# Four matmuls on a tile of ones ahead of the first loaded block

## The chip, the cores and the metric

The kernel runs on one core of a Trainium2 chip. The metric is the device time of one execution in microseconds (us), and the median over executions is compared. One further execution is recorded by the hardware profiler; its times are what the views of the profile show. The engines are named as in the profile: PE (TensorE matmuls), PEld (TensorE weight loads, which overlap PE), DVE (VectorE), ACT (ScalarE), POOL (GpSimd) and SP (SyncE, which here only issues DMAs). A trailing q (SPq, ACTq) is an engine's instruction queue.

## The reference

The input x has 32 batches of 128 tokens with 128 features, in float32. Two layers are added to it, each a conditioned mixture of experts followed by a feed-forward part:

```
x = x + L0_ffn(L0_cond(x, cond))   # L0_cond: top 2 of 4 experts per batch, plus a shared expert
                                   # L0_ffn: 8 gated experts, all used, weighted per token
x = x + L1_ffn(L1_cond(x, cond))   # L1_cond: 2 shared experts, top 2 of 8 experts per token
                                   # L1_ffn: low rank (32) two-layer network
```

What matters around the change is the very first part that is computed, the shared expert of L0_cond:

```
shared = gelu(context_c @ sw1 + sb1, approximate=True) @ sw2 + sb2
```

with `sw1` of 128x512 and `sw2` of 512x128. All matrix products are done in float32.

## The kernel before

The tokens are held transposed, features on the 128 partitions, as eight blocks of 512 tokens (`NB`, `TB`). Two big SBUF tiles hold them for the whole run: `xall` for x and `c0all` for the output of L0_cond; `xT[b]` and `c0T[b]` are their slices of 512 columns. PSUM is one tile `banks` of eight banks of 512 columns. The first six (`NM`) are handed out in turn by `mm_tile`, the last two (`NY`) by `y_tile`; banks 6 and 7 hold sums over several matmuls.

The program first issues its loads, most on the SP queue and three on the ACT queue. The ones that matter here are at L156 to L163:

- L156 (ACT): the first 128 columns of `sw1`; L157 (SP) and L159 (ACT): the two halves of block 0 of x.
- L160 (SP): the other columns of `sw1`; L161 (ACT): `par`, one tile with all small constants and biases.
- L162 (SP): block 1 of x; L163 (SP): `sw2`; L165: blocks 2 to 7. After these come the weights of the later stages.

The work then goes block by block through `pipelined`, which starts the upward part of one unit before the downward part of the unit ahead of it:

- `shared_up(blk)`, L274: four chunks, each a matmul of 128x128 weights by 512 tokens (L279) into its own bank, evicted by ScalarE with gelu and a bias from `par` (L280). For the first two blocks VectorE also sums x over tokens (`sums`, L237), four blocks each.
- `shared_down(blk)`, L286: four matmuls that accumulate in one of banks 6 and 7 (L290), and an eviction by VectorE into `c0T[blk]` (L294).

In between, at points that the table `between` (L639) names, the gates of the conditioned experts are computed (`cond_gates`, L301; `schedule`, L350; `spread_slots`, L411). They are chains of small VectorE operations with small TensorE and ScalarE steps, and their result decides which expert weights are fetched (L471) and used by the 36 units of `unit_up` and `unit_down` (L514 to L546). Then come the eight-expert part (L714 to L761, matmuls L253 and L750), which is most of the time, and layer 1.

POOL fills the last columns of `c0all` (from block 5 on) with zeros at L651, and other constant tiles at L184 to L194. The program says what is to be done in what order on each engine, but a planner may reorder instructions of one engine unless they are kept in program order (`tc.keep_in_program_order`); it also derives from the tiles' regions who waits for whom. TensorE's first instruction in this kernel is the weight load of L279 for block 0.

Of the kernel before, what the change touches and what calls it, by code (L numbers as in the profile page):

```python
# [32 lines left out]
F32 = mybir.dt.float32  # L33
# [5 lines left out]
P = 128  # L39
B, S, D = 32, 128, 128  # L40
BB = 4
TB = BB * S
NB = B // BB
# [6 lines left out]
NHEAD = S // 3  # L50
# [48 lines left out]
def adaln_ffn(  # L99
# [3 lines left out]
    nc = tc.nc  # L103
    V = nc.vector
# [3 lines left out]
    apool = ctx.enter_context(tc.tile_pool(name="acts", bufs=1))  # L108
# [5 lines left out]
    NM, NY = 6, 2  # L114
    banks = psum.tile([P, NM + NY, TB], F32, tag="banks", name="banks", bufs=1)
# [18 lines left out]
    def const(shape, name, dtype=F32):  # L134
        return cpool.tile(shape, dtype, tag=name, name=name)


    par = const([P, NCOLS], "par")
    par32 = const([P, NCOLS32], "par32")
    rows = const([P, NROW], "rows")  # L140
# [3 lines left out]
    wu_t = wpool.tile([P, EF, H], F32, tag="wu", name="wu_t")  # L144
    wd_t = wpool.tile([P, EF, NC, D], F32, tag="wd", name="wd_t")


    xall = apool.tile([P, NB * TB + NHEAD], F32, tag="x", name="xall")
    c0all = apool.tile([P, NB * TB + NHEAD], F32, tag="c", name="c0all")
    xT = [xall[:, b * TB : (b + 1) * TB] for b in range(NB)]  # L150
    c0T = [c0all[:, b * TB : (b + 1) * TB] for b in range(NB)]
    ident = const([P, P], "ident")
# [1109 lines left out]
```

## Time and profile before

| What | Before |
|---|---|
| median of 3 runs | 967.09 us |
| lowest and highest run | 967.04 and 967.91 us |
| the profiled execution, its own time | 966.89 us |
| its span, first to last instruction | 965.1 us |
| time around the span | 1.79 us |
| PE busy | 951.8 us in 6138 passes |
| DVE busy | 593.5 us |
| ACT busy | 351.7 us |
| first matmul starts | 4.54 us |

A row of a timeline gives the start of a group of equal instructions, the time from its first start to its last end, the engine, the line of the code, what is written from what, the shape and the count. In brackets stands the idle time of the engine just before it and what ended that. Ends of matmuls are modelled, so the spacing of starts tells more than a duration does. A float32 matmul appears as two matmul instructions, each with a weight load; they are called passes here. In the window tables each row is a stretch of the span with the busy time and the count of instructions of each engine, the granted TensorE clock as a share of full speed, and the load of the DMA engines.

### The profile page before, as it was taken

To read this page: it belongs to the slowest core of one execution; us is meant where nothing else is said; L and a number is where in the kernel's file an instruction comes from. 1 tells how busy PE (TensorE), PEld (TensorE's weight loads), DVE (VectorE), ACT (ScalarE), POOL (GpSimd) and SP (SyncE) were. 2 spreads that over 40 slices of the span, in tenths; PEclk is the share of its full clock that TensorE was granted. 3 is DMA by queue.
4 is the path that set the end of the run, shared out by engine and by line. 5 is a ranking of instruction groups with operands and counts; after the bars stand their busy time and mean duration, and the time that the engine had idled before them with its cause. 6 is when DMAs were issued, how large, how long until landed. Compare 5 with 4: busy or idle time off the path is not lost.

```text
span 965.1 us, 15705 instructions
## 1 busy us (share of the span) xinstructions
PE 951.8 (99%) x6138; PEld 444.3 (46%) x6138; DVE 593.5 (61%) x1118; ACT 351.7 (36%) x622; POOL 75.1 (8%) x86
## 2 busy tenths in 40 slices
PE   8999999999999999999999999999999999999997
PEld 3588984444444444444444444444444443322333
DVE  4444574766866776686676887668667655633323
ACT  5355544223322322232232332223223223456674
POOL 0000001200101011010101011011010000000000
PEclk9999999999999999999999999999999999999999
DMA  9745641000000000000000000000000003040101
GB/s 315 245 143 171 213 138 48 2 1 4 1 1 2 1 1 1 1 1 1 2 2 1 1 2 3 1 2 1 1 1 1 1 1 89 1 91 1 45 2 45
DMA packets 22850, 38.13 MB, mean 40 GB/s; under 512 B 1968, under 2 KB 13232, under 8 KB 22768
## 3 DMA queue, kind: packets, MB, share of 16 engines
q1 hardware_dynamic: 22192, 36.48, 12.4%
q8 instruction: 53, 0.87, 0.4%
q10 hardware_dynamic: 576, 0.54, 0.2%
q14 instruction: 29, 0.24, 0.1%
HBM read 34.65 MB, written 2.36 MB: 38 GB/s over the span
## 4 chain that ended last, share of the span: by engine, by line
PE 84%; ACT 1%; DVE 0%; issue 0%; DVEq 0%; ACTq 0%
PE banks L253 57%; PE banks L750 20%; PE banks L890 3%; PE banks L290 1%; PE banks L984 1%; ACT hl L992 0%; PE banks L279 0%; PE banks L553 0%; PE banks L266 0%; PE banks L568 0%; PE banks L582 0%; DVE pg L978 0%; DVE pT L979 0%; ACT hs L280 0%; DVE fin L1176 0%
## 5 line engine op out<-in xcount | busy, mean ns | idle before, releaser
L667 ACT ACTIVATE sf<-banks 128x512 f32<-128x512 f32 x256 | 152.7, 597 | 435.3 <-PE banks L253 421.4
L668 DVE TENSOR_TENSOR hf<-sf,banks 128x512 f32<-128x512 f32 x256 | 174.8, 686 | 183.0 <-PE banks L253 182.2
L253 PE MATMUL banks<-c0all,wg_t 128*64 128x512 f32 x1024 | 263.5, 593 | 0.0
L253 PE MATMUL banks<-cg,wu_t 128*64 128x512 f32 x1024 | 263.1, 592 | 0.0
L253 PEld LDWEIGHTS banks<-cg,wu_t 128*64 128x64 f32 x1024 | 73.4, 137 | 146.3 <-issue 126.9
L253 PEld LDWEIGHTS banks<-c0all,wg_t 128*64 128x64 f32 x1024 | 72.8, 137 | 121.4 <-issue 108.8
L662 POOL PARTITION_BROADCAST fg<-fgT x64 | 72.7, 1149 | 655.1 <-DVE cg L711 493.6
L750 PE MATMUL banks<-t,wd_t 128*64 128x256 f32 x512 | 121.0, 379 | 0.0
L750 PE MATMUL banks<-hf,wd_t 128*64 128x256 f32 x512 | 104.2, 379 | 0.0
L750 PEld LDWEIGHTS banks<-hf,wd_t 128*64 128x64 f32 x512 | 53.4, 137 | 55.4 <-issue 36.8
L750 PEld LDWEIGHTS banks<-t,wd_t 128*64 128x64 f32 x512 | 70.1, 137 | 0.0
L524 ACT ACTIVATE h<-banks,w 128x256 f32<-128x256 f32 (+3 forms) x136 | 49.6, 433 | 49.4 <-PE banks L521 49.3
L750 PE MATMUL banks<-hf,a_sum 128*64 128x256 f32 x512 | 66.1, 379 | 0.0
L750 PE MATMUL banks<-t,a_sum 128*64 128x256 f32 x256 | 65.7, 379 | 0.0
L730 DVE TENSOR_TENSOR hf<-hf 128x512 f32<-128x512 f32 x64 | 63.0, 984 | 2.2
L253 PE MATMUL banks<-xall,rw_t 128*32 128x512 f32 x512 | 58.4, 593 | 0.2 <-ACT hl L992 0.2
L253 PE MATMUL banks<-xall,sws 128*32 128x512 f32 x512 | 57.4, 593 | 0.2 <-ACT hl L992 0.2
L537 PE MATMUL banks<-h,w 128*128 128x256 f32 (+3 forms) x272 | 52.5, 338 | 0.0
L521 PE MATMUL banks<-x,w 128*128 128x256 f32 (+3 forms) x272 | 52.2, 337 | 0.0
L521 PEld LDWEIGHTS banks<-x,w 128*128 128x128 f32 x272 | 45.3, 190 | 4.4 <-issue 1.0
L537 PEld LDWEIGHTS banks<-h,w 128*128 128x128 f32 x272 | 44.7, 190 | 4.1 <-issue 0.7
L965 ACT ACTIVATE hr<-banks 128x512 f32<-128x512 f32 x64 | 36.9, 591 | 25.6 <-PE banks L253 25.4
(211 smaller groups left out, 775.1 us busy)
## 6 DMA issues: line engine op xcount, KB each, us to landing
w<-in_experts SPq DMA_DIRECT2D x36, 514.5 KB
wg_t<-in_w_gate SPq DMA_DIRECT2D x8, 256.0 KB
wu_t<-in_w_up SPq DMA_DIRECT2D x8, 256.0 KB
wd_t<-in_w_down SPq DMA_DIRECT2D x8, 256.0 KB
gates<-rg SPq DMA_DIRECT2D x4, 512.0 KB
gates<-rg SPq DMA_DIRECT2D x8, 256.0 KB
xall<-in_x SPq DMA_DIRECT2D x7, 256.0 KB
out<-fin SPq DMA_DIRECT2D x6, 256.0 KB
```

The lines of the kernel that those rows point to most:

```text
L253: mm = nc.tensor.matmul(ps[own, :], lhsT=w[:, own], rhs=x, start=True, stop=True)
L290: nc.tensor.matmul(y, lhsT=sw2_t[:, c, :], rhs=h[:, c, :], start=(c == 0), stop=(c == NC - 1))
L521: nc.tensor.matmul(ps[c][:, :m, :n], lhsT=w1, rhs=x[:, :m, :n], start=True, stop=True)
L524: nc.scalar.activation(h[:, c, :m, :n], ps[c][:, :m, :n], AF.Gelu_apprx_tanh, bias=bias)
L537: nc.tensor.matmul(y[:, :m, :n], lhsT=w2, rhs=h[:, c, :m, :n], start=(c == 0), stop=(c == NC - 1))
L662: nc.gpsimd.partition_broadcast(bc, row)
L667: silu = nc.scalar.activation(s, ps_gate, AF.Silu)
L668: V.tensor_tensor(h, s, ps_up, ALU.mult)
L730: V.tensor_tensor(b12, b12, b11, ALU.subtract)
L750: nc.tensor.matmul(y[half, n], lhsT=w[:, c, :], rhs=h[:, c, :], start=first, stop=(e == EF - 1 and last))
L890: in_order(nc.tensor.matmul(y[32 * j : 32 * (j + 1)], lhsT=w, rhs=h, start=first, stop=last))
L965: in_order(nc.scalar.activation(h[:, at, :], ps, AF.Gelu))
```

## The change

Ahead of all loads in the program, the two tiles `xall` and `c0all` are allocated (they were allocated a few lines further down), VectorE writes ones into the first 256 columns of `c0all`, and TensorE multiplies them four times: the weights are the first 128 of these columns, the moving side all 256, and the result goes to the first half of PSUM bank 7 (`NM + 1`). Nobody reads it. The first real matmul into bank 7, in the second block's `shared_down`, starts a new sum. The 256 columns of `c0all` are later overwritten with the real values by L294.

```diff
+    xall = apool.tile([P, NB * TB + NHEAD], F32, tag="x", name="xall")
+    c0all = apool.tile([P, NB * TB + NHEAD], F32, tag="c", name="c0all")
+
+    V.memset(c0all[:, : TB // 2], 1.0)
+    for _ in range(4):
+        nc.tensor.matmul(
+            banks[:, NM + 1, : TB // 2], lhsT=c0all[:, :P], rhs=c0all[:, : TB // 2], start=True, stop=True
+        )
+
     par = const([P, NCOLS], "par")
...
-    xall = apool.tile([P, NB * TB + NHEAD], F32, tag="x", name="xall")
-    c0all = apool.tile([P, NB * TB + NHEAD], F32, tag="c", name="c0all")
     xT = [xall[:, b * TB : (b + 1) * TB] for b in range(NB)]
```

## The prediction

> **What bounds the kernel now.** I read the page first: the span, busy times and slices.
>
> ```profile
> span 965.1 us, 15705 instructions
> PE 951.8 (99%) x6138; PEld 444.3 (46%) x6138; DVE 593.5 (61%) x1118; ACT 351.7 (36%) x622; POOL 75.1 (8%) x86
> PEclk9999999999999999999999999999999999999999
> ```
>
> TensorE is busy for 951.8 of 965.1 us. Of the 13.3 us of idle time the view of PE's waits puts 4.5 us in one place, the first matmul, which waits for the first block of x. Whatever shortens TensorE's stream anywhere shortens the whole, unless a later wait is tied to something that does not move with it. So I went next to the first microseconds, in the timeline (start, duration, engine, line, operands; in brackets the idle time before and what ended it).
>
> ```profile
> 0.73 0.19 POOL L184 MEMSET ones<- 32x128 f32 x1 [0.29 <-POOLq L1248]
> ...
> 1.00 1.40 POOL L651 MEMSET c0all<- 128x1578 f32 x1
> ...
> 4.50 0.33 DVE L237 TENSOR_REDUCE hd<-xall 128x4 f32<-128x168 f32 x1 [4.50 <-DMA xall<-in_x]
> 4.51 0.50 PEld L279 LDWEIGHTS banks<-xall,sw_t 128*128 128x128 f32 x2 [4.51 <-issue]
> 4.54 7.79 PE L279 MATMUL banks<-xall,sw_t 128*128 128x512 f32 x13 [4.54 <-DMA xall<-in_x]
> ```
>
> Engines are released from the start barrier at about 0.73 us. From then to 4.50 VectorE and TensorE have nothing to do: the gap that the change fills. Then the timeline of the weight loads alone, for the pace of the first real matmuls. A float32 matmul goes as two passes, each with one weight load, and in the steady stream a load starts when the pass before it starts.
>
> ```profile
> 5.53 0.34 PEld L279 LDWEIGHTS banks<-xall,sw_t 128*128 128x128 f32 x1 [0.52 <-issue]
> 6.38 0.34 PEld L279 LDWEIGHTS banks<-xall,sw_t 128*128 128x128 f32 x1 [0.52 <-issue]
> 7.23 0.34 PEld L279 LDWEIGHTS banks<-xall,sw_t 128*128 128x128 f32 x1 [0.52 <-issue]
> 8.09 0.34 PEld L279 LDWEIGHTS banks<-xall,sw_t 128*128 128x128 f32 x1 [0.52 <-issue]
> 8.73 0.19 PEld L279 LDWEIGHTS banks<-xall,sw_t 128*128 128x128 f32 x1 [0.31 <-issue]
> 9.16 0.19 PEld L279 LDWEIGHTS banks<-xall,sw_t 128*128 128x128 f32 x1 [0.24 <-issue]
> 9.59 0.19 PEld L279 LDWEIGHTS banks<-xall,sw_t 128*128 128x128 f32 x1 [0.24 <-issue]
> ```
>
> The pace is 0.853 us a pass up to 8.09 and 0.429 from 8.73 on: half speed, then full. The pass from 8.09 to 8.73 took 0.64, so it is about half of each, and the rise is at 8.09 + 0.42 = 8.51. The first pass began at 5.53 - 0.853 = 4.68, so TensorE worked 3.83 us at half speed and **lost 1.92 us**. Check: the 17th load is at 13.02, so fifteen passes took 8.34 us, where 15 x 0.429 = 6.44; the difference is 1.90. The PEclk row says full speed all along, so it doesn't show this; it does show a fall at the other end, in the table of windows (width, PE busy, PEld, DVE, ACT, POOL, PEclk, DMA):
>
> ```profile
> 964.00:964.50 0.50, 0.00 (x0) 0.00 (x0) 0.00 (x0) 0.00 (x0) 0.00 (x0) 0.74 0.00 0
> 964.50:965.10 0.60, 0.00 (x0) 0.00 (x0) 0.00 (x0) 0.00 (x0) 0.00 (x0) 0.50 0.00 0
> ```
>
> An idle TensorE goes back to exactly half; 0.74 is 0.24 us at full and 0.26 at half speed, so the fall is at 964.24, 3.6 us after the last matmuls began to drain (960.68).
>
> **The change part by part.** Nothing is removed. Added are one VectorE memset of 128x256 and four float32 matmuls of 256 columns, that is eight weight loads and eight passes (6138 + 8 of each). Two tiles are allocated earlier, with no instruction.
>
> *The memset.* VectorE is idle until 4.50, so it is hidden. No VectorE memset is in the trace. Below, it can't be less than 0.14 us, what L333 takes for 32x4; above, 0.43, what L597 takes for two inputs of 128x256. Nearest are one-input rows: 0.22 for 128 columns (L214), 0.18 for 32 (L307), so about 0.0005 us a column, and some 0.29 for 256. I take 0.3. TensorE follows a VectorE result by 0.06 us (L1030 ends at 959.91, the load that waits for it starts at 959.97), and a first pass follows its load by 0.17 (4.51 to 4.68). So the first dummy pass begins at t = 0.73 + 0.3 + 0.06 + 0.17, about **1.25** (1.10 to 1.40 with both ends).
>
> *The eight passes.* At full speed a 256-column pass takes 0.216 (L521: eight in 1.73, 45.17 to 46.90), half of a 512-column one; at half speed I take half of 0.853, 0.427. Eight are 3.41 us, with loads of 0.34 beside them. They end at 4.66, where the first real pass begins anyway at 4.68. Their cover is the wait for x. Each microsecond by which they run past 4.68 is a microsecond of delay; without any cover they would cost 3.41.
>
> *The clock.* If full speed comes 3.83 us after TensorE's first pass, it now comes at 1.25 + 3.83 = 5.08. Of the real work only 4.68 to 5.08 is slow, a loss of 0.20 in place of 1.92: **a gain of 1.7 us**. With t = 1.10 the loss is 0.13; with 1.40 the dummies end 0.13 late and the loss is 0.34. So the gain is 1.6 to 1.8, never over 1.92.
>
> [...]
>
> *What is late next.* Evictions of the first chunks start at 8.92, tied to a load (par, 7.38) and a table load, and do not move. The seventh chunk reuses the first PSUM bank: it would start at about 4.68 + 0.2 + 12 x 0.429 = 10.03, and that bank is free at 8.92 + 0.69 = 9.61. Margin 0.4. Block 1 of x is there at 7.20 (a VectorE sum starts then) and wanted at 8.3. The second chunk's weights were there by 5.53, when their load ran at its normal spacing, and are now wanted at about 5.3: at most 0.2 lost. After that I found no PE wait on a start-anchored load: the 0.9 us at 146 waits for ScalarE, the waits behind 940 are chains of TensorE, VectorE and ScalarE, and all move together. So what is gained at 5 us should reach the end.
>
> *The sum.* The profiled execution took 966.89 us (span 965.1 and 1.79 around it): 966.89 - 1.7 = 965.2. The median of the runs shown is 967.09, 0.2 above it: 967.09 - 1.7 = **965.4**, or 0.18% less. Those runs reach from 967.04 to 967.91, and I let the new ones spread as much.
>
> **The rivals.**
>
> 1. *Nothing gained, 967.1.* The slow passes come from something that the dummies don't touch. The DMA engines are loaded while the first passes run, so a memory port could slow them. Against: DMA share is 1.03 in both 4.5 to 8.5 (slow) and 8.5 to 12.5 (fast) by the windows table, and the factor is almost exactly two. Or constant data doesn't raise the clock; the trace holds no such matmul, so it neither bears this out nor excludes it. Chance 0.09.
>
>    *The moment is missed, also 967.1.* The rise may be bound to set moments and to how full the time between two of them was. The rise at 8.51 then stays, if the dummies begin too late for the moment before it. That gives 966.9 in the profiled execution, and 967.1 for the median. [...] For it speaks that the rise came 3.83 after the start of work, and one rise can't tell a set moment from a set delay. Chance 0.06.
> 2. *The dummies become the delay.* TensorE runs in order, and all dummies stand behind the memset. With first dummy pass at t above 1.27 the real work starts t - 1.27 late, and the loss is t - 1.06; it equals today's 1.92 at **t = 2.98**, beyond which the kernel is slower. The place for that is VectorE's queue: if the memset were put behind the sums of block 0, which wait for x until 4.50 and take 0.8, then t = 5.3 + 0.3 + 0.06 + 0.17 = 5.8, loss 4.8, time 967.1 + 2.9 = 970.0. Against: the memset is written ahead of all of VectorE's work and has no input.
> 3. *The order of later instructions shifts.* VectorE's trace isn't in program order everywhere (L433 runs before L322), so a planner sorts, and TensorE work in front may move its choices. The waits it could touch are the PE idle time outside the first wait, 8.8 us in all; I allow 2 us either way, 963.4 or 967.4.
>
> **How the numbers follow.** Chances: forecast 0.70; rival 1 0.15, its two halves 0.09 and 0.06; rival 2 0.07; rival 3 0.08, half each way. Some 0.2% (1.9 us) is about what a measurement of this kernel can tell from no change, and the forecast lies just inside it: a quarter of its chance, 0.18, goes beyond by scatter of the runs. With half of rival 3, faster is 0.22. Slower is rival 2 and most of the other half of 3, 0.10. The rest, 0.68, is same. The range takes the forecast with the runs' spread (964.7 to 966.3) and reaches up over rival 1 to 967.2; left out are rival 2 and the far ends of 3.
>
> **What would show it.** Right: eight passes on bank 7 between about 1.2 and 4.7, the first real pass still at 4.7, weight loads of L279 at 0.43 spacing from about 5.1 on, and the first load of L290 at 11.3 in place of 13.02; from there every time 1.7 us earlier to the end. Wrong, rival 1: a spacing of 0.85 up to 8.5 again. Rival 2: L279 starting after 4.7. Rival 3: an equal gain at 13 us that is not there at 960.

## The result and the profile after

| What | Before | After |
|---|---|---|
| median of 22 runs each | 967.07 us | 965.55 us |
| lowest and highest run | 966.37 and 967.93 | 965.04 and 966.19 |
| profiled execution, its own time | 966.89 | 965.12 |
| its span | 965.1 | 963.4 |

The ratio is 0.9983, with a 95% interval of 0.9977 to 0.9990: 1.5 us less. The first page of the kernel after:

```profile
span 963.4 us, 15722 instructions
PE 953.5 (99%) x6146; PEld 446.5 (46%) x6146; DVE 594.3 (62%) x1119; ACT 351.5 (36%) x622; POOL 74.8 (8%) x86
```

TensorE is busy 1.7 us longer than before and the span is 1.7 us shorter. The view counts the dummy passes with 3.64 us (their line is below), which lie where TensorE had been idle; so nearly 2 us of busy time went elsewhere, the slow passes. Work that fills an idle stretch is no cost, so a busy time that grows says nothing by itself. The timeline of the start (start, duration, engine, line, what is written from what):

```profile
0.85 0.27 DVE L143 MEMSET c0all<- 128x256 f32 x1 [0.85 <-PEq L1257]
...
1.18 3.06 PEld L145 LDWEIGHTS banks<-c0all 128*128 128x128 f32 x8 [1.18 <-DVE c0all L143]
1.18 3.64 PE L145 MATMUL banks<-c0all 128*128 128x256 f32 x8 [1.18 <-DVE c0all L143]
...
4.80 0.33 DVE L246 TENSOR_REDUCE hd<-xall 128x4 f32<-128x168 f32 x1 [3.67 <-DMA xall<-in_x]
```

The memset takes 0.27 us and the first dummy load follows at 1.18. The first pass is put 0.17 later, at 1.35: its start in the view is modelled, but the second load starts at 1.35 and the others follow every 0.427 us, half speed. In this execution block 0 of x arrives at 4.80, later than in the one before (4.50). The weight loads of the real matmuls, now line L288, then L299:

```profile
4.81 0.30 PEld L288 LDWEIGHTS banks<-xall,sw_t 128*128 128x128 f32 x2 [0.57 <-issue]
5.34 0.19 PEld L288 LDWEIGHTS banks<-xall,sw_t 128*128 128x128 f32 x1 [0.24 <-issue]
5.77 0.19 PEld L288 LDWEIGHTS banks<-xall,sw_t 128*128 128x128 f32 x1 [0.24 <-issue]
...
9.21 0.19 PEld L288 LDWEIGHTS banks<-xall,sw_t 128*128 128x128 f32 x1 [0.24 <-issue]
9.83 0.42 PEld L288 LDWEIGHTS banks<-xall,sw_t 128*128 128x128 f32 x2 [0.44 <-ACT hs L289]
10.49 0.19 PEld L288 LDWEIGHTS banks<-xall,sw_t 128*128 128x128 f32 x1 [0.24 <-ACT hs L289]
...
11.35 0.19 PEld L299 LDWEIGHTS banks<-hs,sw_t 128*128 128x128 f32 x1 [0.24 <-DMA ident<-in_eye]
```

The spacing is 0.43 from the first pass on: no real pass runs at half speed. The first load of the second stage (L290 before, L299 now) moved from 13.02 to 11.35, by 1.67 us. That is about the 1.92 of slow passes, less 0.23 by which the first real pass starts later (5.34 - 0.43 = 4.91 in place of 4.68). The last group of matmuls, before and after:

```profile
959.97 0.31 PEld L984 LDWEIGHTS banks<-qT,par 32*128 32x128 f32 x8 [1.10 <-DVE qT L1030]
958.23 0.31 PEld L993 LDWEIGHTS banks<-qT,par 32*128 32x128 f32 x8 [1.10 <-DVE qT L1039]
```

It starts 1.74 earlier, so nothing was given back on the way.

When did the clock rise? The windows table at the end of the kernel after (width, PE busy, PEclk, DMA share, GB/s) shows where it fell again:

```profile
960.00:960.50 0.50, 0.00 (x0) 0.77 0.22 80
```

0.77 is 0.27 us at full and 0.23 at half speed, so the fall is at 960.27. Before, rise and fall lay 955.73 us apart (8.51 and 964.24); taken off here, that gives a rise at 4.54, in the last dummy pass. The prediction had 5.08. The trace's own record of the clock confirms it. That record begins with the rise, which is why the clock column reads full speed ahead of it, and it has full speed from 8.51 before and from 4.54 after, for 955.73 us in both.

### The profile page after: what moved, and what is told of

The parts are those of the page before. It is cut to its first block, busy times and chain, and to the rows that moved or that the text cites. A ratio compares the mean times of both kernels' runs of the same rounds, so it can differ in the third digit from the quotient of the medians.

```text
span 963.4 us, 15722 instructions
## 1 busy us (share of the span) xinstructions
PE 953.5 (99%) x6146; PEld 446.5 (46%) x6146; DVE 594.3 (62%) x1119; ACT 351.5 (36%) x622; POOL 74.8 (8%) x86
## 4 chain that ended last, share of the span: by engine, by line
PE 84%; ACT 0%; DVE 0%; issue 0%; DVEq 0%; ACTq 0%
PE banks L262 57%; PE banks L759 20%; PE banks L899 3%; PE banks L299 1%; PE banks L993 1%; ACT hl L1001 0%; PE banks L288 0%; PE banks L562 0%; PE banks L275 0%; PE banks L577 0%; PE banks L591 0%; DVE pg L987 0%; DVE pT L988 0%; DVE fin L1185 0%; DVE qT L1039 0%
```

## The experiments

Theory A, a guess that the runs are to try: the clock rises when TensorE was busy enough in the time up to some moment, and the dummies bring that moment forward. The expectations call this time a window. How full it has to be is what the runs are to tell; for its length they give one number, 3.41 us, by which full speed lasted longer with eight dummies than in the other profiles (959.14 and 955.73 us). Each run below was timed beside the kernel before on the same chip, whose median is given with it.

**The memset alone** (the loop of dummies taken out).

> The earlier allocation and the memset alone, without the four matmuls. [...] Rival B (the gain comes from the earlier allocation or the memset, that is from a changed order or layout): 965.5 us, as with the whole change.

Measured: 967.24 against 967.25, ratio 1.000 (0.9991 to 1.0009), and loads at 0.85 spacing from 5.53 to 8.09 once more. Allocation and memset gain nothing, so the matmuls are the cause.

**How many: two, three, eight** (`range(4)` to `range(2)`, `range(3)`, `range(8)`).

> Two dummy matmuls in place of four: four passes, 1.35 to 3.06 us, then TensorE idle for about 1.7 us until x lands. Theory A with windows that must be full: no window is filled sooner than without dummies, so 967.1 us. Theory A with windows that need be only half full: up to 1.7 us gained, 965.5 to 966.2 us. Rival C (busy time is added up, wherever it lies): the rise comes 1.7 us earlier, half of it is gained, 966.2 us.

> Three dummy matmuls: six passes, 1.35 to 3.91 us, then idle for about 0.8 us until x lands. A window that takes in the gap is 77% full. Theory A with full windows: nothing or little gained, 966.8 to 967.1 us. Theory A with windows that may be three quarters full: the whole gain, 965.5 us. Rival C (busy time is added up): the rise comes 2.6 us earlier, 965.8 us.

> Eight dummy matmuls, twice as many. [...] The loss against an ideal start is 1.8 to 3.5 us, that of before 1.7 to 3.4, so 967.1 to 967.3 us: the gain is eaten. If passes past the loads cost nothing (because real loads are late anyway): 965.5 us. If they cost their half-speed time: 965.5 + 3.4 = 968.9 us.

Measured beside 967.25: two 967.35 (0.9997, 0.9988 to 1.0006), three 965.43 (0.9985, 0.9976 to 0.9994), eight 967.42 (0.9999, 0.9990 to 1.0008). Two bring nothing, so busy time isn't simply added up (rival C falls). Three bring as much as four, although TensorE idles before x arrives. Weight loads with three:

```profile
1.18 2.21 PEld L145 LDWEIGHTS banks<-c0all 128*128 128x128 f32 x6 [1.18 <-DVE c0all L143]
4.42 0.50 PEld L288 LDWEIGHTS banks<-xall,sw_t 128*128 128x128 f32 x2 [1.04 <-issue]
5.32 0.19 PEld L288 LDWEIGHTS banks<-xall,sw_t 128*128 128x128 f32 x1 [0.40 <-issue]
5.75 0.19 PEld L288 LDWEIGHTS banks<-xall,sw_t 128*128 128x128 f32 x1 [0.24 <-issue]
```

The first real pass goes from 4.59 (0.17 after its load) to 5.32. That is 0.73, neither 0.85 (slow) nor 0.43 (fast): it was slow for about 0.6 and the rise is at 5.20. The fall gives the same, for the window from 960.50 shows it at 960.93:

```profile
960.50:961.00 0.50, 0.00 (x0) 0.93 0.83 287
```

960.93 - 955.73 = 5.20. The 3.41 us that end there hold 1.78 to 3.91 of dummies and 4.59 to 5.20 of real work, 2.74 us: they were 80% busy, and the clock rose. That is one execution; of the eleven with three, two gained nothing, 967.65 and 967.69.

With eight the dummies push the real work back:

```profile
1.18 4.85 PEld L145 LDWEIGHTS banks<-c0all 128*128 128x128 f32 x16 [1.18 <-DVE c0all L143]
6.05 0.41 PEld L288 LDWEIGHTS banks<-xall,sw_t 128*128 128x128 f32 x2
6.70 0.19 PEld L288 LDWEIGHTS banks<-xall,sw_t 128*128 128x128 f32 x1 [0.24 <-issue]
```

The real passes are all fast but start at 6.70 - 0.43 = 6.27, which is 1.6 later than before. The gain is eaten, as expected.

**Two longer ones** (`range(2)`, 320 columns).

> Two dummy matmuls of 320 columns: four passes of 0.53 us, 1.4 to 3.5 us, between two and three of 256 columns in time, with the instruction count of two. The runs with two (no gain; its window was 48% full) and with three (whole gain; 80% full) put the share that a window must be full between these. Here a window that takes in the whole gap up to 4.6 us is 68% full. If the threshold is at about half: 965.5 us; if at about three quarters: 966.5 to 967.2 us, with part of the executions gaining all and part nothing. If the number of instructions counts and not the time: 967.2 us, as with two.

Measured: 967.08 against 967.30 (0.9998, 0.9989 to 1.0007). No gain, where the expectation had 965.5 us for a threshold at about half. Whether the time of the dummies or their number falls short, this run can't tell; the one with two of 512 columns below can. Its loads:

```profile
8.94 0.34 PEld L288 LDWEIGHTS banks<-xall,sw_t 128*128 128x128 f32 x1 [0.52 <-issue]
9.79 0.28 PEld L288 LDWEIGHTS banks<-xall,sw_t 128*128 128x128 f32 x1 [0.52 <-issue]
10.31 0.19 PEld L288 LDWEIGHTS banks<-xall,sw_t 128*128 128x128 f32 x1 [0.24 <-issue]
```

The pass from 9.79 took 0.52, so it was slow for 0.17 and the rise is at 9.96. One length of 3.41 us earlier, at 6.55, the clock did not rise, and the 3.41 us up to there, from 3.14 on, were 67% busy (0.41 of dummies, 1.87 of real work).

**Zeros in place of ones** (`V.memset(..., 0.0)`), and **both once more**.

> Four dummy matmuls on a tile of zeros in place of ones. Theory A (what counts is that TensorE is busy): the whole gain, 965.5 us, as with ones. Rival D (what counts is switching in the array, so that constant data counts little): zeros switch nothing, the clock rises as late as before, 967.2 us.

> The changed kernel itself once more, beside the one with zeros on the same chip: 965.5 us. Theory A has both alike within 0.2 us; if data matter, they lie apart by 0.4 us as in the two earlier measurements.

> The kernel with zeros once more, beside the one with ones: by theory A 965.5 us, within 0.2 us of it; if zeros are better, 965.15 us again.

Measured: zeros 965.15 against 967.30 (0.9977, 0.9968 to 0.9987); then, side by side with 967.54 before, ones 965.30 (0.9980, 0.9971 to 0.9989) and zeros 965.52 (0.9983, 0.9974 to 0.9992). The 0.4 us between the first two measurements did not come back. Rival D falls: the zeros gained 2.15 and 2.02 us and the ones, beside the second, 2.24.

The second profile of the ones is of the longest of its eleven executions, 966.24 us:

```profile
4.44 0.65 PEld L288 LDWEIGHTS banks<-xall,sw_t 128*128 128x128 f32 x2 [0.20 <-issue]
5.61 0.34 PEld L288 LDWEIGHTS banks<-xall,sw_t 128*128 128x128 f32 x1 [0.52 <-issue]
6.46 0.34 PEld L288 LDWEIGHTS banks<-xall,sw_t 128*128 128x128 f32 x1 [0.52 <-issue]
7.31 0.19 PEld L288 LDWEIGHTS banks<-xall,sw_t 128*128 128x128 f32 x1 [0.51 <-issue]
7.74 0.19 PEld L288 LDWEIGHTS banks<-xall,sw_t 128*128 128x128 f32 x1 [0.24 <-issue]
```

The same program, and the real passes up to 7.3 are slow: the rise is at 7.29. One length of 3.41 us earlier, at 3.88, the clock did not rise, and the 3.41 us up to there, from 0.47 on, were 74% busy (1.35 to 3.88).

**Narrower dummies, and fewer, wider ones** (`[:, :224]`; `range(2)` with 512 columns).

> Four dummies of 224 columns instead of 256: eight passes of 0.373 us, 1.35 to 4.33 us, so that they end ahead of the earliest arrival of x seen so far (4.4 us) and never delay it. The gap that is left, 0.2 to 0.6 us, keeps every window over 82% full, and the runs so far put the threshold between 67% and 80%. Theory A: the whole gain and none of the delay, 965.2 to 965.5 us. If windows must be fuller than that: 966 to 967 us.

> Two dummies of 512 columns in place of four of 256: four passes of 0.853 us, the same time on TensorE with half of the instructions. The memset is twice as wide, some 0.14 us longer. Theory A (time counts): 965.5 to 965.7 us. If instructions or weight loads are counted: 966.5 to 967.2 us.

Measured beside 967.54: 224 columns 965.72 (0.9981, 0.9972 to 0.9990), two of 512 965.79 (0.9982, 0.9973 to 0.9991). Two wide dummies gain what four do, where two of 256 or 320 columns gained nothing. So with four passes each, 3.41 us of them (4 x 0.853) gained 1.75 us, and 1.7 us (4 x 0.427) or 2.1 (4 x 0.53) gained nothing that can be told: in these runs the time on TensorE made the difference, not the number of instructions. Ending ahead of x brings nothing that can be told from the changed kernel, and no version was clearly faster than it.

**Dummies that come late** (`V.memset(c0all[:, : 3 * TB], 1.0)`, and `5 * TB`).

> The memset is made six times as wide (1536 columns), so that the same four dummies start late. By its width the memset takes 0.9 to 1.6 us, the first dummy pass begins at t = 2.0 to 2.7 us, and the dummies run past the arrival of x. By the prediction's formula for late dummies the loss is t - 1.06, that is 0.9 to 1.6 us against 1.92: 966.2 to 967.0 us. If late dummies cost nothing: 965.5 us. If the clock's window is missed: 967.2 us and the delay of 0.7 to 1.4 us on top, 968 to 968.6 us.

> The memset is made ten times as wide (2560 columns); the planner then puts the four dummies behind the first real matmul, where nothing covers them. The real work starts with x as before, so the clock rises as late as before, and the eight passes add their full-speed time, 8 x 0.216 = 1.7 us, wherever the rise falls: 968.9 us against 967.2. The prediction's figure for dummies without cover was 3.41 us (all at half speed): 970.6 us. If they are hidden even there, behind evictions: 967.2 us.

Measured beside 967.30: 966.56 (0.9992, 0.9983 to 1.0001) and 968.82 (1.0015, 1.0006 to 1.0024). In the first the dummies begin at 2.68, for which the formula t - 1.06 gives a loss of 1.6 against 1.92, 967.0. Measured is 0.7 less than before, in an interval from 1.6 less to 0.1 more: some of the gain seems to be left, and how much these runs don't tell. In the second the dummies run after the first real matmul:

```profile
5.24 2.05 PE L288 MATMUL banks<-xall,sw_t 128*128 128x512 f32 x2 [5.24 <-DMA xall<-in_x]
7.08 3.24 PE L145 MATMUL banks<-c0all 128*128 128x256 f32 x8
```

The same eight passes, out of their cover, cost 1.5 us. Expected were 1.7.

In the kernels with three, eight, two of 512 and late dummies the planner also moved a few later matmuls; what that is worth was not tried by itself. The others have TensorE's matmuls in the order of the kernel after.

**All fourteen profiles together.** The trace's record of the clock gives the rise of each, and it agrees with the spacing of the loads wherever a real pass shows it. Full speed lasts 955.73 us in thirteen of them, wherever the work began, and 959.14 with eight: 3.41 more. No fixed delay after TensorE's first pass fits: the rise came 3.83 after it before (4.68 to 8.51), 3.19 in the profile after (1.35 to 4.54) and 5.94 in the second profile of the ones (1.35 to 7.29). That rise and fall keep to moments 3.41 us apart is an estimate from the two lengths; one such step was measured, in one profile. Two terms then give the time of each profiled execution. To 964.97 us, the time for no loss at all (966.89 - 1.92), come the start of the first real pass less 4.68, and half of the time from that start to the rise, where the rise is later. For the dummies behind the first real matmul, their 1.73 us at full speed (8 x 0.216) come on top.

| Profile | first real pass | rise | sum | measured |
|---|---|---|---|---|
| after | 4.91 | 4.54 | 965.20 | 965.12 |
| three | 4.59 | 5.20 | 965.18 | 965.24 |
| two of 512 | 5.03 | 7.07 | 966.34 | 966.35 |
| four, second profile | 4.76 | 7.29 | 966.32 | 966.24 |
| eight | 6.27 | 4.31 | 966.56 | 966.47 |
| 1536 columns | 6.09 | 7.00 | 966.84 | 966.76 |
| two | 4.82 | 9.08 | 967.24 | 967.27 |
| two of 320 | 4.68 | 9.96 | 967.61 | 967.62 |
| 2560 columns | 5.38 | 9.80 | 969.61 | 969.50 |

The kernel before is the one by which the 964.97 is set; the four profiles that are not listed are no further off than 0.09. That leaves little for moved matmuls in the profiled executions. In the last row 0.7 us are x, which came at 5.21 in that execution.

## Why the prediction was right, point by point

- *The bound and the place.* Right. What was gained at 11 us was still there at 958.
- *The number.* Forecast 965.4, measured 965.55, inside the range. The prediction held that some 0.2% is what a measurement can tell; with 22 runs each it was finer, 0.07% either way.
- *The dummies.* Right. First pass at 1.35 against 1.25, and inside the range. They end about when x arrives. That x came at 4.80 in the profile after is scatter between executions: it came at 4.51 with the memset alone, 4.42 with three dummies and 4.38 with eight.
- *The half-speed passes are the clock, not the DMA.* Right. In the kernel after the first dummy pass ran at half speed, 1.35 to 1.77, while the DMA engines moved nothing (share 0.00 up to 1.70), and the real passes ran at full speed with the DMA engines loaded (1.02 from 4.91 to 8.50).
- *"If full speed comes 3.83 us after TensorE's first pass."* This step was wrong, without harm to the sum. It came 3.19 after it in the profile after, 5.9 after it in the second profile of the ones. What stays the same is how long full speed lasts. With three, with two of 320 and in the second profile of the ones, rise (by the spacing) and fall (by the clock column: 960.93, 965.69, 963.03) lie 955.7 apart as before. With eight, sixteen dummy passes took 4.92 us (1.35 to 6.27), which at 0.427 and then 0.216 each puts the rise at 4.3; the fall is at 963.46, 959.1 later. That the sum held all the same is luck in the sizes: the dummies start 4.68 - 1.35 = 3.33 earlier than the real work did, nearly the 3.41 by which the two lengths of full speed differ. So a fixed delay and, by the estimate above, moments 3.41 apart both bring the rise about 3.4 us forward, and half of that is 1.7. In the two profiles it moved by 3.97 (8.51 to 4.54).
- *How busy TensorE was ahead of the rise.* The shares of TensorE's busy time in 3.41 us, and whether the clock rose at their end:

| Profile | from and to, us | busy | rise |
|---|---|---|---|
| before | 1.69 to 5.10 | 12% | no |
| two | 2.25 to 5.66 | 48% | no |
| two of 512 | 0.24 to 3.65 | 60% | no |
| two of 320 | 3.14 to 6.55 | 67% | no |
| four of 224 | 0.41 to 3.82 | 74% | no |
| four, second profile | 0.47 to 3.88 | 74% | no |
| three | 1.78 to 5.20 | 80% | yes |
| four of zeros | 0.70 to 4.11 | 81% | yes |
| eight | 0.90 to 4.31 | 87% | yes |
| four, first profile | 1.13 to 4.54 | 94% | yes |

  (Passes are counted from 0.17 after their first load, at 0.427 us each for 256 columns. The 3.41 us end at the rise where the table says yes, and 3.41 ahead of the rise where it says no; the rise is taken from the fall, 955.73 earlier, and 959.14 earlier with eight.) Where the table says no, the next 3.41 us were busy throughout, with four of 224 for 89%, and the clock rose at their end. So in these ten profiles it rose after a share of 80% or more, and not after one of 74% or less. The share alone doesn't place the rise: in the second profile of the ones TensorE was busy from 1.35 on, and the clock rose only at 7.29.
- *A gain of 1.7.* Measured 1.5, and 2.2 when the same kernel was measured once more (967.54 to 965.30). The intervals reach from 1.0 to 2.2 and from 1.1 to 2.8, so both allow 1.7. The scatter can come from where the moment falls. An estimate from the step of 3.41 (with eight), a share of 77% (between the 74% and the 80% of the table) and the first passes at 4.68 and 1.35, for moments 3.41 apart at any position: a start at 4.68 brings the rise between 7.3 and 10.7, a loss of 1.3 to 3.0, mean 2.2; a start at 1.35 brings it between 4.0 and 7.4. Where that is ahead of the real work, at about 4.76, part of the head start buys nothing. The mean loss is then 0.6, and the gain 1.6. With 964.97 for no loss at all the runs should lie in 966.3 to 968.0 before and 965.0 to 966.4 after; they lie in 966.4 to 967.9 and 965.0 to 966.2. That the moments keep this spacing and that their position is spread evenly is argued from this fit, not shown.
- *What is late next.* Right, but it was close. In the profile after, the load at 9.83 came 0.2 late because it waited for ScalarE, of the 0.24 that it had to spare; the next ones are back at the old spacing (9.21 + 3 x 0.43 = 10.50, seen 10.49), so no pass was late.
- *The rivals.* Nothing gained: fell. The moment is missed: a late rise is seen, but not at its price. In the second profile of the ones the rise came at 7.29 where the first had it at 4.54, with the first pass at 1.35 in both. That execution, 966.24, is still shorter than any of the kernel before (the shortest of all took 966.28). That the rise is bound to set moments was not shown by itself. Dummies as delay: real, and priced by the eight and the late ones. For the eight the expected loss of 1.8 to 3.5 us, and 1.7 to 3.4 before, took a range for the place of the rise that no run shows; the profiles have rises at 4.31 and 8.51, and losses of 1.5 (966.47 - 964.97) and 1.92. The form of this rival with the memset behind VectorE's sums arose in no run; where the memset was longest the planner moved the dummies behind real work instead. "Without any cover they would cost 3.41" was mis-sized: 1.5 were measured, about their time at full speed (1.7). In the profile with 2560 columns the rise came at 9.80, while the dummies ran (7.08 to 10.16), and their 1.73 at full speed bring its sum to 969.61 of 969.50 measured. Order shifted: not in this change; TensorE's matmuls are in the order of before but for the added ones.

## What to carry to other kernels

If the first matmuls of a trace run at twice the spacing of later ones, and TensorE idled ahead of them while inputs were loading, dummy matmuls in that idle stretch are worth a try. Here they gained 1.5 of 967 us, of the 1.92 that 3.83 us at half speed had cost. In these runs the clock rose after 3.41 us in which TensorE was 80% busy or more, and not after 74% or less. Two dummies (1.7 us) brought nothing (967.35 beside 967.25), and eight, which ran 1.6 past the start of the real work, cost what they gained (967.42). Compare medians of many runs: single profiled executions of the changed kernel took 965.12 and 966.24. Read the speed from the spacing of weight loads: before, the clock column read 1.00 from 4.5 to 8.5, where the passes ran at half speed.

## What the runs showed of the hardware

- Part of the scatter of this kernel's times has a place: the same program ran its first real passes fast in one profile (965.12 us, rise at 4.54) and slow up to 7.3 in another (966.24).
- Dummies on a tile of zeros gained as those on a tile of ones did (965.52 and 965.30 side by side, 967.54 before).
- A VectorE memset of float32 takes 0.27 us for 256 columns and 2.19 for 2560, some 0.8 ns a column; the prediction's 0.5 ns from one-input rows was low.
- The clock did not fall only after 3.41 us without any work. In the profile after it fell at 960.27, and in the 3.41 us up to there the view has 1.47 us of small matmuls; before it has 0.00 and with eight 0.23. In the 3.41 us ahead of these, at whose end the clock did not fall, it has 2.31, 2.65 and 2.52.
